# A two-layer graph network on one core: conv 1's weight product of the first graph in native float32, and another order of head and tail

## The chip, the cores and the metric

The kernel runs on one core of a Trainium2 chip. The metric is device time in microseconds (us) of one execution, here the median of three runs. The core has five engines that run side by side, each with its own instruction list, in order: TensorE (PE, matrix products into the PSUM banks; PEld is its loading of the stationary operand), VectorE (DVE), ScalarE (ACT), GpSimd (POOL) and SyncE (SP), which here only issues DMAs. They wait for one another by semaphores.

## The reference

There are 128 graphs of 128 nodes with 512 features (`x`), each with a 128x128 matrix `adj`. Two layers run one after the other.

```python
# layer 0
h = relu(layernorm(x))
x = x + (conv(layernorm(relu(conv(h, W1, b1))) * gamma + beta, W2, b2) + h)
# conv(h, W, b): H = (adj != 0); w = first row of adj
#   Dn = 1 / (H @ w);  Be = 1 / H.sum(axis=1)
#   Dn * (H @ (Be * (H.T @ (h @ W.T)))) + b
# layer 1
h = relu(layernorm(x))
x = x + relu(concat(h, (adj @ h) / rowsum(adj)) @ W.T)
```

W1 is 1024x512, W2 is 512x1024, W is 512x1024, all float32.

## The kernel before, in words

Each graph is one tile of 128 partitions, so the work is 128 graphs through a long pipeline of small steps. Each step is a Python function with the graph's number `g` (and sometimes a half), and issues one to some ten instructions. The order of the steps is written out by hand: `head()` lists the start, where graphs 0 to 4 enter and the weights are loaded and prepared; `step(s)`, for s from 3 to 124, is the steady loop, in which seven graphs stand at different points; `tail()` lists the end. The order of the list is the order in which each engine gets its instructions. An engine in front of an instruction that cannot start yet holds all that is behind it in its own list, and nothing else.

The steps that matter here, by graph:

- `load_x`, `load_adj`, `load_adjb`, `load_w1`, `load_w2`, `load_w3`, `load_bias` issue DMAs, all on SP except graph 0's `load_adjb`, which is on ACT. `load_adjb` loads adj in four pieces of rearranged 32x32 blocks. `load_affine` issues eight small DMAs on POOL.
- `incidence` (DVE: transpose, then not-equal), `incidence_count`, `incidence_weight`, `incidence_inverse`, `incidence_high` (ACT, then DVE, L419), `incidence_scale` (two parts), `node_matrix` (one matmul and ACT's copy) and `node_sum` (DVE) make the node operator S = H Be H^T of a graph, and its degrees. `node_floor`, `node_scale`, `node_up` make their inverse, in `dinv`.
- `x_sums`, `x_spread`, `scales`, `shifts`, `x_norm` are the layer norm of x, in `h0`; `residual` and `residual_bias` add to x on POOL.
- `conv1_nodes` multiplies S from the left, in native float32 (128 columns, eight instructions), into PSUM, `pz`.
- `conv1_high`, `conv1_low`, `conv1_rest` split `pz` into three parts `z`, and `conv1_weights(g, half)` multiplies by one half of W1. `conv1_main` (ACT) and `conv1_out` (DVE) take the two PSUM banks out into `r`, `conv1_bias` adds b1.
- `inner_sums`, `inner_spread`, `inner_norm` are the inner layer norm; `inner_out`, `inner_in`, `inner_turn` transpose `r` by way of DRAM (`n_scratch`, `nb`) and DVE; `inner_high`, `inner_low`, `inner_rest` split the result.
- `conv2_weights`, `conv2_main`, `conv2_weights_out`, `conv2_bias` (to `g`), `conv2_nodes` (to `py`), `conv2_out` finish layer 0. The `layer1_*`, `mean_*` and `aggregate` steps are layer 1, `finish` stores the graph.

Most products are split: a float32 value is written as a high and a low part in the format `fp32r`, and a third part `d` for the correction, so that one product takes three groups of matmuls (`product`, L521). Each half of a weight is a `Half`, 128 partitions x 4 x 512. `high(i)` (ACT, L179) and `low(i)` (DVE, L183) make the parts from the loaded values `raw`, two of the four blocks at a time, and `rest(i)` makes `d` from the two:

```python
            self.raw = const.tile([P, KD, 512], FP, tag=name + "d", name=name + "r")
...
                self.d = const.tile([P, KD, 512], FP, tag=self.name + "d", name=self.name + "d").bitcast(FR)
...
                eng.tensor_tensor(self.d[:, c], self.l[:, c], self.h[:, c], SUB)
```

So `d` takes the memory of `raw` (the same tag), and can be written only when `raw` has been read for the last time. On DVE `rest` is one instruction (L195), on POOL four, and without an engine it is a pair of matmuls with a unit matrix and a copy on ACT for each block (L199 to L201). The weights' names in the trace are `w10`, `w11`, `w20`, `w21`, `w30`, `w31`, with `r`, `h`, `l` or `d` behind them.

`beta_row(k)` (L262) is eight native float32 matmuls in all, of 512 columns, into one PSUM bank, which `beta_out` reads; `scale_w2(k)` then scales that block of W2 in place. `fill(768)` puts matmuls of 768 columns that nobody reads in front of the next use of a PSUM bank; in the head that is `conv1_nodes(0)`.

There are six PSUM banks for products, and two for `ps_s`, `pz` and `py`.

Of the kernel before, what the change touches and what calls it, by code (L numbers as in the profile page):

```python
# [7 lines left out]
FP = mybir.dt.float32  # L8
# [12 lines left out]
DOWN_12 = 2.0**-12  # L21
# [3 lines left out]
def gnn_kernel(  # L25
# [485 lines left out]

    @stage
    def conv1_low(g):
        PZ[g][0]()
# [430 lines left out]
    def head():  # L945
        load_w1(0, 0)
        load_adjb(0, nc.scalar)
        load_x(1)
        incidence(0)
        copy(eps_root, eps, AF.Sqrt)  # L950
        load_affine()
        load_x(0)
        incidence_weight(0, nc.gpsimd)
        incidence_count(0, nc.vector)
        load_w1(0, 1)
        incidence_inverse(0)
        x_sums(1, "A")
        x_sums(0)
        w1[0].high(0)
        w1[0].high(1)  # L960
        load_x(2)
        load_w1(1, 0)
        w1[0].low(0)
        incidence_high(0)
        x_spread(0)
        scales(0, 1)
        incidence_scale(0, 0, nc.gpsimd)
        incidence_scale(0, 1, nc.scalar)
        load_w1(1, 1)
        w1[0].low(1)  # L970
        w1[0].rest(1, nc.vector)
        load_adjb(1)
        shifts(0, 1, nc.gpsimd)
        x_norm(0)
        node_matrix(0)
        fill(768)
        w1[1].high(1)
        load_w2(0)
        node_sum(0)
        incidence(1)  # L980
        conv1_nodes(0)
        w1[1].high(0)
        residual(0)
        node_floor(0, nc.vector)
        incidence_count(1, nc.vector)
        load_adjb(2)
        w1[0].rest(0, nc.vector)
        x_spread(1)
        load_bias(b2_bc, b2)
        load_bias(b1_bc, b1)  # L990
        w1[1].low(1)
        incidence_inverse(1)
        conv1_high(0)
        conv1_low(0)
        conv1_rest(0)
        node_scale(0)
        incidence_weight(1, nc.gpsimd)
        conv1_weights(0, 0)
        incidence_high(1)
        w1[1].low(0)  # L1000
        incidence_scale(1, 0, nc.scalar)
        w1[1].rest(0, nc.vector)
        incidence_scale(1, 1, nc.scalar)
        load_adj(0)
        node_up(0, nc.scalar)
        conv1_main(0, 0)
        scales(1, 1)
        load_w2(1)
        node_matrix(1)
        shifts(1, 1, nc.gpsimd)  # L1010
        incidence(2)
        node_sum(1)
        incidence_count(2, nc.gpsimd)
        beta_row(0)
        conv1_out(0, 0)
        w1[1].rest(1, nc.vector)
        x_sums(2)
        beta_row(1)
        conv1_weights(0, 1)
        incidence_weight(2, nc.vector)  # L1020
        node_floor(1, nc.gpsimd)
        x_spread(2)
        scale_w2(0, nc.vector)
        scales(2, 1)
        x_norm(1)
        beta_row(2)
        load_x(3)
        shifts(2, 1, nc.gpsimd)
        incidence_inverse(2)
        conv1_bias(0, 0, nc.vector)  # L1030
        scale_w2(1, nc.scalar)
        w2[0].high(0)
        beta_row(3)
        incidence_high(2)
        conv1_nodes(1)
        load_adjb(3)
        scale_w2(2, nc.vector)
        conv1_main(0, 1)
        load_w3(1)
        mean_operator(0)  # L1040
        node_scale(1)
        scale_w2(3, nc.scalar)
        incidence_scale(2, 0, nc.vector)
        incidence_scale(2, 1, nc.scalar)
        w2[0].high(1)
        conv1_out(0, 1)
        residual_bias(0)
        conv1_high(1, True)
        node_matrix(2)
        conv1_bias(0, 1, nc.vector)  # L1050
        beta_row(4)
        beta_row(5)
        x_norm(2)
        node_sum(2)
        conv1_nodes(2)
        mean_degree(0, nc.vector)
        node_up(1, nc.gpsimd)
        node_floor(2, nc.vector)
        inner_sums(0)
        inner_spread(0)  # L1060
        residual(1)
        node_scale(2)
        residual(2)
        load_adjb(4)
        conv1_low(1)
        scale_w2(5, nc.vector)
        scale_w2(4, nc.vector)
        conv1_high(2)
        incidence(3)
        incidence_weight(3, nc.gpsimd)  # L1070
        conv1_rest(1)
        incidence_count(3, nc.gpsimd)
        scales(0, 2)
        incidence_inverse(3)
        conv1_low(2)
        beta_row(6)
        shifts(0, 2, nc.vector)
        beta_row(7)
        w2[1].high(0)
        conv1_rest(2)  # L1080
        incidence_high(3)
        w2[0].low(1)
        unit()
        scale_w2(6, nc.vector)
        inner_norm(0)
        x_sums(3)
        scale_w2(7, nc.scalar)
        w2[0].low(0)
        mean_inverse(0)
        w2[1].low(0)  # L1090
        node_up(2, nc.scalar)
        incidence_scale(3, 0, nc.vector)
        w2[1].high(1)
        conv1_weights(1, 0)
        conv1_weights(1, 1)
        incidence_scale(3, 1, nc.scalar)
        conv1_main(1, 0)
        conv1_main(1, 1)
        inner_out(0)
        w2[0].rest(0)  # L1100
        inner_in(0)
        conv1_out(1, 0)
        x_spread(3)
        w2[0].rest(1)
        conv1_out(1, 1)
        conv1_bias(1, 0, nc.vector)
        conv1_bias(1, 1, nc.vector)
        inner_sums(1)
        node_matrix(3)
        conv1_weights(2, 0)  # L1110
        scales(3, 1)
        incidence(4)
        w2[1].low(1)
        inner_spread(1)
        w2[1].rest(1, nc.gpsimd)
        incidence_weight(4, nc.vector)
        load_x(5)
        inner_turn(0)
        beta_out()
        scales(1, 2)  # L1120
        conv1_weights(2, 1)
        incidence_count(4, nc.gpsimd)
        inner_high(0)
        shifts(1, 2, nc.scalar)
        node_sum(3)
        inner_norm(1)
        w3[1].high(1)
        w3[1].high(0)
        load_x(4)
        shifts(3, 1, nc.gpsimd)  # L1130
        inner_low(0, nc.vector)
        load_w3(0)
        incidence_inverse(4)
        inner_rest(0)
        x_norm(3)
        w2[1].rest(0, nc.vector)
        incidence_high(4)
        conv2_weights(0)
        mean_scale(0, nc.scalar)
        conv1_nodes(3)  # L1140
        conv2_main(0)
        conv1_main(2, 0)
        conv1_main(2, 1)
        incidence_scale(4, 1, nc.scalar)
        inner_out(1)
        conv2_weights_out(0)
        conv1_high(3, True)
        inner_in(1)
        x_sums(4)
        residual_bias(1)  # L1150
        conv2_bias(0, nc.vector)
        conv1_out(2, 0)
        conv1_low(3)
        conv1_rest(3)
        incidence_scale(4, 0, nc.scalar)
        inner_turn(1)
        conv2_nodes(0)
        conv2_out(0)
        residual(3)
        w3[0].high(1)  # L1160
        load_adjb(5)
        residual_bias(3)
        x_spread(4)
        scales(4, 1)
        conv1_weights(3, 0)
        mean_out(0)
        inner_high(1)
        residual_bias(2)
        conv1_out(2, 1)
        layer1_sums(0)  # L1170
        conv1_bias(2, 0)
        conv1_bias(2, 1, nc.vector)
        layer1_spread(0)
        inner_low(1, nc.vector)
        scales(0, 3)
        shifts(0, 3, nc.vector)
        inner_sums(2)
        inner_rest(1)
        load_adj(1)
        w3[0].low(1)  # L1180
        shifts(4, 1, nc.gpsimd)
# [379 lines left out]
```

## Time and profile before

| | |
|---|---|
| median of 3 runs | 2447.64 us (2446.86 to 2447.76) |
| the profiled execution | 2447.67 us |
| its span, first to last instruction | 2445.9 us |
| busy: PE, PEld | 2422.7, 2009.6 us |
| busy: DVE, ACT, POOL | 2298.1, 2009.9, 1324.8 us |
| granted TensorE clock | 1.0 of full speed |
| first matmul | 11.40 us |
| first product of graph 0 | 16.88 us |
| first product of graph 1 | 31.94 us |
| first product of the steady loop | 70.94 us |
| one steady step | 18.75 us |
| last DMA issued | 2442.54 us |

In a row of the profile, `L530 PE MATMUL rm<-w10h,z` is a matmul of line 530, which writes `rm` and reads `w10h` and `z`; a number behind x counts instructions, and in an order of time the two first columns are start and length in us. Times of matmuls overlap, since they are pipelined: what counts is the distance from start to start. A wait is given as who waited, for whom, with the total, the count and the longest.

### The profile page before, as it was taken

The page shows a single profiled execution, that of the slowest core. Times are in us where ns is not written, and L with a number is a line of the kernel's source. Part 1 is how long each engine was busy: PE and PEld are TensorE (multiplying, and loading weights), DVE is VectorE, ACT ScalarE, POOL GpSimd, SP SyncE. Part 2 cuts the span into 40 slices and gives each one's busy share as a digit, 9 for nine tenths or more (in the row PEclk, how much of TensorE's full clock was granted, in tenths as well). Part 3 has the DMA queues.
Part 4 walks back from the last instruction along what each step waited for, and adds up shares of the span by engine and source line. Part 5 has one row for each costly group of instructions (what it writes and reads, how often), then busy time and mean ns, then how long its engine had stood idle before and what let it go on. Part 6 is the DMA issues. An engine that isn't in the chain of part 4 may idle for free.

```text
span 2445.9 us, 41647 instructions
## 1 busy us (share of the span) xinstructions
PE 2422.7 (99%) x11170; PEld 2009.6 (82%) x11170; DVE 2298.1 (94%) x5843; ACT 2009.9 (82%) x4512; POOL 1324.8 (54%) x1808
## 2 busy tenths in 40 slices
PE   7999999999999999999999999999999999999998
PEld 5788888888888888888888888888888888888886
DVE  8899999999999999999999999999999999999987
ACT  8888888888888888888888888888888888888785
POOL 5555555555555555555555555555555555555552
PEclk9999999999999999999999999999999999999999
DMA  6344433344434443444344443434343444344432
GB/s 186 114 129 125 130 124 129 124 130 128 129 119 130 132 126 123 129 129 127 124 128 128 126 129 123 132 123 130 122 133 121 130 127 131 119 131 131 127 124 92
DMA packets 408956, 311.39 MB, mean 127 GB/s; under 512 B 176656, under 2 KB 339984, under 8 KB 408720
## 3 DMA queue, kind: packets, MB, share of 16 engines
q1 hardware_dynamic: 407888, 308.66, 40.1%
q8 instruction: 88, 1.44, 0.2%
q14 instruction: 148, 1.21, 0.2%
q10 hardware_dynamic: 576, 0.07, 0.0%
q0 software_dynamic: 256, 0.01, 0.0%
HBM read 166.21 MB, written 142.34 MB: 126 GB/s over the span
## 4 chain that ended last, share of the span: by engine, by line
PE 95%; ACT 2%; DVE 1%; DMA 1%; issue 1%; SPq 0%; POOL 0%; POOLq 0%; DVEq 0%; ACTq 0%
PE gm L530 19%; PE rm L530 18%; PE am L530 9%; PE bm L530 9%; PE gd L535 9%; PE rd L535 9%; PE bd L535 5%; PE ad L535 5%; PE pz L488 4%; PE am L832 2%; PE ad L832 1%; PE ym L743 1%; PE yd L744 1%; PE ym L742 1%; PE ps_s L430 1%
## 5 line engine op out<-in xcount | busy, mean ns | idle before, releaser
L306 ACT ACTIVATE h<-x_t 128x512 f32<-128x512 f32 x255 | 159.1, 624 | 291.8 <-DVE x_t L754 283.8
L81 POOL TENSOR_TENSOR r<-r,b_bc 128x256 f32<-128x256 f32 x500 | 358.7, 739 | 70.1 <-DVE r L555 54.4
L300 POOL TENSOR_SCALAR st<-st 128x1 f32<-128x1 f32 x130 | 82.3, 633 | 569.9 <-DVE st L317 563.2
L81 POOL TENSOR_TENSOR hl<-ht,hh 128x256 fp32r<-128x256 f32 x250 | 235.4, 963 | 216.5 <-ACT hh L612 216.5
L81 POOL TENSOR_TENSOR x_t<-x_t,h 128x256 f32<-128x256 f32 x256 | 239.8, 959 | 1.3 <-ACT h L326 1.1
L81 POOL TENSOR_TENSOR g<-g,c 128x256 f32<-128x256 f32 x246 | 177.6, 743 | 72.4 <-DVE g L694 72.4
L326 ACT ACTIVATE h<-x_t,st 128x512 f32<-128x512 f32 x255 | 206.1, 808 | 2.0 <-POOL st L300 1.2
L555 DVE SCALAR_TENSOR_TENSOR r<-rd,dinv,r 128x512 f32<-128x512 f32 x256 | 190.8, 746 | 7.7 <-ACT r L550 6.3
L81 POOL TENSOR_TENSOR x_t<-x_t,b_bc 128x256 f32<-128x256 f32 x256 | 187.2, 752 | 0.0
L311 ACT ACTIVATE h<-x_t,st 128x512 f32<-128x512 f32 x255 | 182.9, 717 | 4.1
L550 ACT ACTIVATE r<-rm,dinv 128x512 f32<-128x512 f32 x256 | 174.7, 684 | 7.7 <-PE rm L530 4.4
L694 DVE SCALAR_TENSOR_TENSOR g<-gd,g 128x512 f32<-128x512 f32 x127 | 87.8, 691 | 79.5 <-issue 70.4
L621 DVE SCALAR_TENSOR_TENSOR nd<-nh,nl 128x1024 fp32r<-128x1024 f32 x127 | 155.5, 1225 | 4.2
L326 ACT ACTIVATE r<-r,st 128x1024 f32<-128x1024 f32 x128 | 157.8, 1233 | 0.1
L591 DVE STREAM_TRANSPOSE nt<-nb 128x1024 f32<-128x1024 f32 x127 | 156.9, 1235 | 0.4 <-DMA nb<-n_scratch 0.3
L81 DVE TENSOR_TENSOR nl<-nt,nh 128x1024 fp32r<-128x1024 f32 x127 | 153.5, 1208 | 1.9 <-ACT nh L612 1.7
L530 PE MATMUL am<-w31h,hh 128*128 128x512 f32 x504 | 146.8, 413 | 0.0
L311 ACT ACTIVATE junk<-r,st 128x1024 bf16<-128x1024 f32 x128 | 145.2, 1134 | 0.1
L488 PEld LDWEIGHTS pz<-s,h 128*128 128x128 f32 x1024 | 134.5, 192 | 11.1 <-ACT h L326 0.7
L530 PE MATMUL rm<-w11h,z 128*128 128x512 f32 x512 | 140.3, 396 | 0.0
L530 PE MATMUL rm<-w11l,z 128*128 128x512 f32 x512 | 139.3, 393 | 0.0
L530 PE MATMUL rm<-w10h,z 128*128 128x512 f32 x512 | 138.2, 392 | 0.9 <-ACT z L501 0.9
(244 smaller groups left out, 7594.1 us busy)
## 6 DMA issues: line engine op xcount, KB each, us to landing
n_scratch<-r SPq DMA_DIRECT2D x128, 512.0 KB, 2.6
nb<-n_scratch SPq DMA_DIRECT2D x508, 128.0 KB, 2.8
x_t<-in_x_dram SPq DMA_DIRECT2D x128, 256.0 KB, 2.7
h_scratch<-h SPq DMA_DIRECT2D x127, 256.0 KB, 2.3
hb<-h_scratch SPq DMA_DIRECT2D x508, 64.0 KB, 1.9
out_dram<-o SPq DMA_DIRECT2D x127, 256.0 KB, 2.0
adj_t<-in_adj_dram SPq DMA_DIRECT2D x128, 64.0 KB, 1.9
an_scratch<-adj_t SPq DMA_DIRECT2D x128, 64.0 KB, 1.6
```

What stands on the lines that cost most here:

```text
L81: eng.tensor_tensor(dst[:, s], a[:, s], b[:, s], op)
L306: copy(junk, src, func, accum_out=t[:, 0:1])
L311: copy(junk, src, AF.Square, bias=t[:, 1:2], accum_out=t[:, 2:3])
L326: copy(dst, src, func, bias=t[:, 5:6], scale=t[:, 4:5])
L488: nc.tensor.matmul(z[:, k * P : (k + 1) * P], H0[g][:, k * P : (k + 1) * P], S[g], start=True, stop=True)
L530: nc.tensor.matmul(pm, left[i](k), right(i, k), start=(i == 0 and k == 0), stop=(i == 1 and k == kk - 1))
L535: nc.tensor.matmul(pd, left[2](k), right(2, k), start=(k == 0), stop=(k == kk - 1), skip_group_check=True)
L550: copy(R[g][:, HALVES[half]], PY.pop((g, half)), AF.Copy, scale=DN[g][:, 1:2])
L555: nc.vector.scalar_tensor_tensor(r, PR.pop((g, half)), dn[:, 0:1], r, MUL, ADD)
L591: nc.vector.transpose(nt.rearrange("p k (i b) -> p k i b", b=B), t.rearrange("p i k a -> p k i a"))
L621: nc.vector.scalar_tensor_tensor(t, h, 2.0**-12, low, MUL, SUB)
L694: nc.vector.scalar_tensor_tensor(G[g], PG.pop(g), 4096.0, G[g], MUL, ADD)
```

## The change

Three functions are new. For graph 0 alone, `native_high` copies `pz` out once, as plain float32, scaled by 2^-12; `native_weights` multiplies it by a half of W1 as loaded (`raw`), four native float32 matmuls of 512 columns into one bank; `native_main` takes that bank out on ACT, with the row scale. They stand for `conv1_high`, `conv1_low`, `conv1_rest`, `conv1_weights`, `conv1_main` and `conv1_out` of graph 0. The four `rest` steps of W1 come behind the native product that reads their half. The parts of W1 are still made for all other graphs. `step(s)` is unchanged.

The order of the other steps in `head()` and `tail()` is new throughout, and some small steps sit on another engine. The diff, cut:

```diff
+    def native_high(g):
+        done.update((v.f, g) for v in (conv1_high, conv1_low, conv1_rest))
+        Z[g] = z = left.tile([P, KD, P], FP, tag="h1", name="z")
+        copy(z.rearrange("p k c -> p (k c)"), PZ.pop(g), AF.Copy, scale=DOWN_12)
+
+    def native_weights(g, half):
+        done.add((conv1_weights.f, g, half))
+        PR[g, half] = b = bank("rn")
+        for k in range(KD):
+            nc.tensor.matmul(b, Z[g][:, k], w1[half].raw[:, k], start=(k == 0), stop=(k == KD - 1))
+
+    def native_main(g, half):
+        done.update((v.f, g, half) for v in (conv1_main, conv1_out))
+        if half == 0:
+            R[g] = pool.tile([P, DH], FP, tag="r", name="r")
+        copy(R[g][:, HALVES[half]], PR.pop((g, half)), AF.Copy, scale=DN[g][:, 0:1])
```

The new head, from its start to the first product of graph 1, with the steps that the text speaks of:

```diff
     def head():
+        load_x(0)
         load_w1(0, 0)
         load_adjb(0, nc.scalar)
+        load_bias(b2_bc, b2)
+        incidence(0)
+        load_affine()
+        w1[0].high(0)
+        w1[0].low(0)
+        incidence_count(0, nc.vector)
+        x_sums(0)
         load_x(1)
...
+        load_w1(1, 0)
+        incidence_weight(0, nc.scalar)
+        scales(0, 1)
         load_w1(0, 1)
+        incidence_high(0)
+        shifts(0, 1, nc.vector)
+        incidence_scale(0, 0, nc.vector)
+        load_adjb(1)
+        incidence(1)
+        incidence_scale(0, 1, nc.scalar)
+        load_x(2)
+        w1[1].high(0)
+        load_w1(1, 1)
         w1[0].high(1)
+        node_matrix(0)
+        node_sum(0)
...
+        fill(768)
+        load_w2(0)
+        conv1_nodes(0)
+        native_high(0)
+        w1[1].high(1)
+        w1[0].low(1)
...
+        native_weights(0, 0)
+        w1[1].low(1)
+        w1[0].rest(0, nc.vector)
+        beta_row(0)
+        incidence_scale(1, 0, nc.scalar)
+        incidence(2)
...
+        beta_row(2)
+        native_weights(0, 1)
+        load_w2(1)
+        w1[0].rest(1, nc.vector)
+        beta_row(3)
+        load_adjb(3)
+        native_main(0, 0)
+        incidence_scale(2, 0, nc.scalar)
+        w2[0].low(0)
+        incidence_scale(2, 1, nc.vector)
+        native_main(0, 1)
+        scale_w2(2, nc.vector)
+        x_norm(2)
+        conv1_bias(0, 0, nc.vector)
+        shifts(1, 1, nc.gpsimd)
+        node_matrix(2)
+        node_sum(1)
+        x_norm(1)
+        conv1_bias(0, 1, nc.vector)
+        conv1_nodes(1)
+        inner_sums(0)
+        residual(2)
         w1[1].rest(0, nc.vector)
...
+        w1[1].rest(1, nc.gpsimd)
...
+        inner_norm(0)
+        unit()
+        inner_out(0)
...
+        beta_out()
         conv1_weights(1, 0)
         conv1_weights(1, 1)
```

Its end, and the places in the tail that the text speaks of:

```diff
+        conv2_weights(1)
...
+        w3[0].rest(1)
+        w3[0].rest(0, nc.gpsimd)
...
+        conv2_nodes(1)
...
+        inner_out(2)
+        inner_in(2)
         load_adjb(5)
         layer1_high(0)
         layer1_low(0, nc.vector)
+        load_adj(1)
+        w3[1].rest(1)
...
+        w3[1].rest(0)
...
     def tail():
...
-        layer1_low(c)
+        layer1_low(c, nc.vector)
...
-        layer1_trip_out(d)
-        mean_in(d)
...
-        layer1_trip_in(d)
+        layer1_trip_out(d)
...
+        layer1_trip_in(d)
...
+        mean_in(d)
...
-        mean_scale(e, nc.vector)
+        mean_scale(e, nc.gpsimd)
```

## The prediction

> **What bounds the kernel now.** I read the page's engine shares first, then the busy times in six stretches, then what TensorE waited for, and last the order of time in the head, the only place besides the tail that the change touches.
>
> The page:
>
> ```profile
> PE 2422.7 (99%) x11170; PEld 2009.6 (82%) x11170; DVE 2298.1 (94%) x5843; ACT 2009.9 (82%) x4512; POOL 1324.8 (54%) x1808
> PE 95%; ACT 2%; DVE 1%; DMA 1%; issue 1%; SPq 0%; POOL 0%; POOLq 0%; DVEq 0%; ACTq 0%
> ```
>
> TensorE is busy 99% and carries 95% of the chain. Time can only come from its 23.2 us without work, or go into more work for it. The stretches (columns: stretch, length, then busy time of PE, PEld, DVE, ACT, POOL, with instructions):
>
> ```profile
> 0.00:11.40 11.40, 0.00 (x0) 0.03 (x1) 2.64 (x10) 6.65 (x15) 6.36 (x15) 1.00 0.80 264
> 11.40:16.88 5.48, 4.54 (x14) 3.12 (x14) 5.32 (x10) 4.35 (x8) 3.51 (x4) 1.00 0.92 206
> 16.88:31.94 15.06, 14.72 (x57) 9.53 (x58) 14.15 (x38) 12.66 (x28) 6.74 (x12) 1.00 0.95 217
> 31.94:70.94 39.00, 36.79 (x156) 27.86 (x154) 35.34 (x62) 37.25 (x79) 19.27 (x28) 1.00 0.44 132
> 70.94:2395.15 2324.21, 2323.86 (x10768) 1936.94 (x10769) 2204.75 (x5661) 1922.87 (x4331) 1279.99 (x1739) 1.00 0.40 127
> 2395.15:2445.90 50.75, 42.80 (x178) 32.06 (x176) 35.86 (x66) 26.12 (x54) 8.88 (x13) 1.00 0.27 88
> ```
>
> 16.88 is the first product of graph 0, 31.94 the first of graph 1, 70.94 the first of the steady loop. From 70.94 to 2395.15 TensorE idles 0.35 us: nothing there can be won. The idle time lies in 0 to 16.88 (12.34), in the rest of the head (0.34 + 2.21) and after 2395 (7.95). In the head DVE (35.34 of 39.00) and ACT (37.25) are nearly as full as TensorE. Its waits, first in 0 to 120 us, then after 2250:
>
> ```profile
> PE ps_s L430 <- ACT sb L298: 11.4, 1, 11.4
> PE py L738 <- DVE g L81: 1.1, 1, 1.1
> PE rm L530 <- ACT z L501: 0.9, 1, 0.9
> ...
> PE py L738 <- POOL w11ds L81: 1.7, 1, 1.7
> PE py L738 <- DVE g L81: 1.0, 1, 1.0
> ```
>
> No product waited for a third part of W1. What the first product waits for is `z`, at the end of the chain adjacency, node matrix, x_norm, conv1_nodes. The durations that the sum uses:
>
> ```profile
> 2.69 1.28 ACT L950 ACT_TABLE_LOAD   x1 [2.69 <-issue]
> 9.52 1.23 DVE L183 SCALAR_TENSOR_TENSOR w10l<-w10h,w10r 128x1024 fp32r<-128x1024 f32 x1
> 11.75 2.76 PE L100 MATMUL pz<-eps 128*128 128x512 f32 x4
> 12.28 1.23 DVE L195 TENSOR_TENSOR w10d<-w10l,w10h 128x1024 fp32r<-128x1024 f32 x1
> 19.88 1.88 PE L262 MATMUL pc<-w20r,gb 128*128 128x512 f32 x4
> 22.53 1.08 PE L530 MATMUL rm<-w11l,z 128*128 128x512 f32 x4
> 23.45 1.09 PE L535 MATMUL rd<-w11d,z 128*128 128x512 f32 x4
> ```
>
> The x4 of L262 are two native matmuls of 512 columns, two instructions each; they start 0.43 apart. The x4 of L530 run from 22.53 to 23.45: 0.23 each.
>
> **The change part by part.**
>
> *The product.* Removed: 24 matmuls by 0.23 = 5.5 us. Added: 8 native ones, 16 instructions by 0.43 = 6.9. All of it is on TensorE's path: **+1.3** (1.1 to 1.6, by the last digits of the two spacings). TensorE's first 4 us run slower: the 512-column filler instructions start 0.85 apart, and conv1_nodes' spacing falls from 0.21 to 0.11 near 15.4. The new product starts after that, as the old one did. The Trainium skill (TensorE: Matmul & The Clock Gate, "What's actually happening") says that the array runs at half rate until a free-running window of about 3.4 us has been busy; by it another phase could leave part of the first native half at double spacing, up to 3.4 us more. This trace shows full speed 4.0 us after the first matmul, and the sum goes by that.
>
> *What goes with it.* DVE loses conv1_low and conv1_rest of graph 0 (0.67 each) and two conv1_out (0.74 each): 2.8 us. ACT's two copies out of PSUM stay (0.68 each). All other steps are the same, on other engines: w1[1].rest(1) (1.23 on DVE) goes to POOL and w2[1].rest(1) comes from POOL to DVE; two conv1_bias (0.67) leave DVE for POOL; small scalings move about. I count DVE 2.5 and ACT 2.0 less in the head, most of ACT's behind 32 us.
>
> *The start.* The x load, W1's quarter, b2 and the other x now stand ahead of the fourth piece of adjb. In the trace the pieces land in order of issue with the other loads (w10 1.5, x 0.65, b2 1.6 us of transfer), the last at 8.44. The new list ahead of it is 0.65 + 1.5 + 1.6 + 0.65 against 1.5 + 0.65 + 0.65 + 1.6: equal, so incidence(0) starts near 8.5 again. Behind it DVE now does w1[0].low(0) (1.2) before the count and the inverse, where before it stood behind them, ahead of L419; and scale(0,0) is a DVE 0.28 instead of a POOL 1.24. Together node_matrix(0) comes at 11.3 (11.40 before). ACT then does two W1 high parts (0.95 each, start to start) ahead of the node matrix's copy and x_norm(0), which ends at 13.8 (before 13.25); the filler ends at 14.2 anyway, so that costs nothing while the filler covers it; without it, 0.5. conv1_nodes 1.5 and z's copy 0.6 put the product at 16.5: **-0.4** (-0.8 if adjb lands earlier; +1.0 if ACT's table is loaded twice, once for the copies now in front of the square root: row 1.28, of which some 0.3 is slack). The Trainium skill (ScalarE: Activation LUTs, "What ACT_TABLE_LOAD costs") prices a switch of table set at about 2.7 us, of which 1.28 is the load. By it the start would be 2.0 later. The trace has one load only, and the page also lists copy among the functions of every set.
>
> *From the product to graph 1's (15.06 before).* A new wait: w1[0].rest(0) writes over the raw half, so it waits for native_weights(0, 0), which ends at 16.5 + 3.4 = 19.9, while DVE is through with w1[1].low(1) near 18. Queued behind it are incidence(2), mean_operator(0), incidence_inverse(2), scales(2, 1); node_matrix(2) and x_norm(2) wait for those. The 1.8 us of idle DVE is covered by the 2.8 that it lost. Then TensorE: beta_row 0.86, node_matrix(1), two beta_rows, the second half 3.4, a beta_row: 26.9. ACT, replayed by these rows, comes to x_norm(1) only at 28.2, behind two sums, two spreads, scale_w2, w2[0].high(0) and the two native copies, so conv1_nodes(1) waits 1.3, where before 0.7 was lost on node_matrix(2): **+0.6**, between -0.7 (no loss) and +2.0. Two conv1_nodes and four beta_rows later graph 1's product starts at 33.4 (31.94 before).
>
> *From there to the loop (39.00 before).* 2.21 us of idle and some slow starts were lost to DVE and ACT: 1.1 before conv2_nodes(0), the rest on banks before and between the W2 and W3 third parts. With ACT 2.0 shorter, beta_out ahead of graph 1's products (its bank free by 33, at 44.4 before) and the W3 parts split around conv2_nodes(1), I take back **-1.4**: about two thirds of the idle, the row that all of it comes from. Ends: -2.2 and +1.5. The upper one holds the late loads: load_adjb(5) and load_adj(1) now stand behind inner_in(2) on SP (issued 69.85 to 71.6 before), would land near 75.3, and incidence(5) stood at 75.17; inner_low(2), behind it on DVE, had 0.7 of slack.
>
> *The tail.* TensorE's order is nearly the same. layer1_low(c) goes from POOL (1.45) to DVE (0.69), and TensorE stood for its output: -0.5. trip_in(d) no longer stands behind mean_in(d), whose four issues took 2.9 on SP: -0.4. The 1.7 for conv2_bias(e) on POOL stays. **-0.9**; ends -2.0 (the 7.95 less the last 5.5, in which only the final chain runs) and +1.5 (mean_scale(e) goes to POOL, and mean_transpose(e) had some 1.5 us to spare).
>
> **Sum.** +1.3 - 0.4 + 0.6 - 1.4 - 0.9 = -0.8, taken as -1.0 with the late digits. The profiled execution took 2447.67 (span 2445.9), which is the median 2447.64 within 0.03; so 2446.7. Changes under 0.2% (4.9 us) are not told from none here.
>
> **The rivals.** *Graph 0 comes late* (slower). The vectors of graph 0 share one chain: native copy, bias, sums, spread, inner_norm(0), trip through DRAM, conv2_weights(0). Before, inner_norm(0) ended at 35.1 and conv2_weights(0) began with 0.1 us of wait. ACT's list between z's copy and inner_norm(0) is 16.1 us of work; from 16.5 with the waits above I get 34.7. Past 36.5 (35.1 plus graph 1's later start) every us goes on TensorE. If the waits for native products cost ACT 8 us instead of 2, it ends near 41: +4.5 - 0.8 + 2, so 2453.4. For it: ACT's queue is strict and x_norm(2), x_norm(1) now stand ahead of inner_sums(0). Against: no wait of 2 us in ACT's list before.
>
> *All gains come in* (faster): -0.8 + 1.1 - 0.7 - 2.2 - 2.0 = -4.6, so 2443.0. For it: each of these is idle time that the stretches show. Against: DVE and ACT are 90% and 96% full in the head, and gaps seldom all close.
>
> *The table is loaded twice or the first transfers come late*: the start at +1.0 instead of -0.4: 2448.1. Against: the first 5 us of ACT are empty.
>
> *The change is no change for TensorE*: were a native product as short as the split one, 1.3 less: 2445.4; L262 speaks against it.
>
> **How the numbers follow.** Forecast 0.62, graph 0 late 0.18, all gains 0.10, start late 0.08, no added work 0.02. Faster takes four fifths of all gains: 0.08. Slower takes four fifths of graph 0 late and a little of the forecast's upper ends: 0.16. Same 0.76. Range: 2443.2 leaves out about 0.08, 2451.5 about 0.12.
>
> **What would show it.** Right: 16 native instructions 0.43 apart for graph 0; first product near 16.5; graph 1's near 33.4; the loop's first layer1_mean near 70.8; the 18.75 us step unchanged; TensorE idle after the loop under 7.5. Wrong: a second ACT_TABLE_LOAD, DVE idle over 2 us in front of w10d, inner_norm(0) ending after 36.5, or a wait of TensorE inside the loop.

## The result, and the profile after

The changed kernel takes 2453.85 us (median of 10 runs, 2452.07 to 2456.06), before beside it 2447.71 (10 runs, 2446.27 to 2450.16). The ratio is 1.0024 with a 95% interval of 1.0016 to 1.0032, so the change costs 3.9 to 7.8 us. The forecast was 2446.7, a little faster than before, with a range of 2443.2 to 2451.5. The profiled execution of the changed kernel took 2453.32 us (span 2451.5), 5.65 more than the profiled execution of before.

Lines after `L515` have moved by 17: `L530` of before is `L547`, `L535` is `L552`, `L550` is `L567`, `L738` is `L755`. First the page of the changed kernel, engine shares and chain:

```profile
PE 2426.5 (99%) x11162; PEld 2007.7 (82%) x11162; DVE 2300.3 (94%) x5854; ACT 2009.2 (82%) x4508; POOL 1318.2 (54%) x1797
PE 94%; ACT 2%; DVE 2%; DMA 1%; issue 0%; SPq 0%; POOL 0%; DVEq 0%; ACTq 0%
```

Then the six stretches between the same events as before (start, node matrix of graph 0, first product of graph 0, first product of graph 1, loop, end; columns as before):

```profile
0.00:11.66 11.66, 0.00 (x0) 0.00 (x0) 2.67 (x11) 7.21 (x17) 4.73 (x12) 1.00 0.70 214
11.66:17.09 5.43, 4.74 (x13) 3.17 (x13) 3.62 (x9) 3.45 (x7) 2.85 (x4) 1.00 0.96 265
17.09:34.34 17.25, 15.88 (x51) 7.96 (x51) 14.14 (x36) 14.78 (x35) 11.71 (x13) 1.00 0.93 205
34.34:74.88 40.54, 37.60 (x157) 27.47 (x155) 37.62 (x69) 36.00 (x72) 21.84 (x31) 1.00 0.43 126
74.88:2400.79 2325.91, 2325.38 (x10768) 1936.91 (x10769) 2205.27 (x5664) 1921.65 (x4328) 1267.78 (x1728) 1.00 0.40 127
2400.79:2451.51 50.72, 42.89 (x178) 32.14 (x176) 36.96 (x68) 26.13 (x55) 9.27 (x12) 0.98 0.28 88
```

Read the second column against that of before: 11.66 for 11.40, 5.43 for 5.48, 17.25 for 15.06, 40.54 for 39.00, 2325.91 for 2324.21, 50.72 for 50.75. So the head costs 3.9 us, the loop 1.7 in these two executions, the tail nothing. TensorE's idle time between graph 1's product and the loop has grown from 2.21 to 2.94. DVE and ACT, which were expected to have less work in the head, are busy 37.62 and 36.00 us there, for 35.34 and 37.25. TensorE's waits in 0 to 120 us (who, for whom, total, count, longest):

```profile
PE ps_s L430 <- ACT sb L298: 11.7, 1, 11.7
PE py L755 <- DVE g L81: 1.7, 2, 1.1
PE pz L488 <- ACT h L326: 1.4, 1, 1.4
PE rn L521 <- ACT z L515: 0.7, 1, 0.7
PE gm L547 <- DVE nl L81: 0.3, 1, 0.3
```

The order of time shows the native product and, behind it, the 1.37 us that conv1_nodes(1) waited for x_norm(1). Of the next stretch it shows ScalarE's 2.14 us without work in front of conv1_main(1, 0):

```profile
17.09 3.70 PE L521 MATMUL rn<-w10r,z 128*128 128x512 f32 x8 [0.69 <-ACT z L515]
23.47 3.60 PE L521 MATMUL rn<-w11r,z 128*128 128x512 f32 x8
29.41 0.82 PE L488 MATMUL pz<-s,h 128*128 128x128 f32 x5 [1.37 <-ACT h L326]
40.67 1.27 ACT L567 ACTIVATE r<-rm,dinv 128x512 f32<-128x512 f32 x2 [2.14 <-PE wd L199]
```

That last row is the lead. conv1_main(1, 0) writes over `r`, which inner_out(0) reads. The bracket names a matmul that had long been done; the other thing it waits for is the DMA of inner_out(0), issued at 35.57 and landed at 40.59. In before the same trip was issued at 35.16 and landed at 37.75.

### The profile page after: what moved, and what is told of

It is laid out like the page before. It is cut to its first block, busy times and chain, and to the rows that moved or that the text cites. A ratio compares the mean times of both kernels' runs of the same rounds, so it can differ in the third digit from the quotient of the medians.

```text
span 2451.5 us, 41621 instructions
## 1 busy us (share of the span) xinstructions
PE 2426.5 (99%) x11162; PEld 2007.7 (82%) x11162; DVE 2300.3 (94%) x5854; ACT 2009.2 (82%) x4508; POOL 1318.2 (54%) x1797
## 4 chain that ended last, share of the span: by engine, by line
PE 94%; ACT 2%; DVE 2%; DMA 1%; issue 0%; SPq 0%; POOL 0%; DVEq 0%; ACTq 0%
PE gm L547 18%; PE rm L547 18%; PE am L547 9%; PE bm L547 9%; PE gd L552 9%; PE rd L552 9%; PE bd L552 5%; PE ad L552 5%; PE pz L488 4%; PE am L849 2%; PE ad L849 1%; PE ym L760 1%; PE ym L759 1%; PE yd L761 1%; PE ps_s L430 1%
## 5 line engine op out<-in xcount | busy, mean ns | idle before, releaser
L567 ACT ACTIVATE r<-rm,dinv 128x512 f32<-128x512 f32 x254 | 173.2, 683 | 13.7 <-DMA n_scratch<-r 5.2
L547 PE MATMUL am<-w31h,hh 128*128 128x512 f32 x504 | 146.6, 413 | 0.0
L547 PE MATMUL rm<-w11h,z 128*128 128x512 f32 x508 | 139.6, 396 | 0.0
L547 PE MATMUL rm<-w11l,z 128*128 128x512 f32 x508 | 138.1, 393 | 0.0
L488 PE MATMUL pz<-s,h 128*128 128x128 f32 x1024 | 135.5, 276 | 1.4 <-ACT h L326 1.4
```

Of the source, the lines that this page charges most:

```text
L488: nc.tensor.matmul(z[:, k * P : (k + 1) * P], H0[g][:, k * P : (k + 1) * P], S[g], start=True, stop=True)
L547: nc.tensor.matmul(pm, left[i](k), right(i, k), start=(i == 0 and k == 0), stop=(i == 1 and k == kk - 1))
L567: copy(R[g][:, HALVES[half]], PY.pop((g, half)), AF.Copy, scale=DN[g][:, 1:2])
```

## The experiments

The kernels were timed in five rounds, in four groups, each beside before on the same chip (before: 2449.6, 2449.4, 2449.1 and 2448.8 us). An interval is about 2 us to either side, so the small terms are read from the profiled executions. The start, up to graph 0's first product, differs by up to 1.6 between them (16.26 to 17.88 us). "Head" is therefore counted from graph 0's first product to the loop: 54.07 us in before and 54.02 in a second execution, 57.79 and 57.86 in the changed kernel.

(In the stretches above, graph 1's product is put 0.03 earlier than its first matmul in before, 31.97, so 15.06 and 39.00 there are 15.09 and 38.98 here.)

**Which part of the change.** Four kernels took the change apart. First, the native product alone, in the order of before:

```diff
-        conv1_high(0)
-        conv1_low(0)
-        conv1_rest(0)
...
+        native_high(0)
...
-        conv1_weights(0, 0)
+        native_weights(0, 0)
```

with native_main for conv1_main, no conv1_out of graph 0, and W1's third parts behind the product.

> Head and tail in the order of before, only graph 0's product native, and W1's third parts behind it. Theory A (the new order of the head costs the time; the product only its 1.3 us on TensorE, with 2.8 us of DVE work gone): 2448.2 to 2449.8 against 2447.7, first product of graph 0 within 0.3 of 16.88, first product of the loop at 71.0 to 73.0. Rival B (the native product, or the third parts waiting behind it, costs the time): 2452 or more, first product of the loop at 74 or later.

Measured: 2453.12 us, ratio 1.0016 (1.0007 to 1.0025), so about +3.5, between the two theories. Its head takes 56.39, 2.32 more than before, and all of that lies between graph 0's product and graph 1's (17.47 instead of 15.09); from there to the loop it is as before (38.92). TensorE's product is 1.4 longer. The rest goes with a wait of 1.6 in front of graph 2's node matrix, for ScalarE's copy of graph 1's `z`; in before the wait at this place was 0.3. (A second wait for a copy of `z`, 1.5 where before had 0.9, lies ahead of graph 0's product and outside this count.)

The new head with the tail of before:

> The changed head with the tail of before. Theory A (all of it in the head, the tail is worth nothing): 2453 to 2454.5, first product of the loop at 74.5 to 75.3. Rival C (the new tail loses what its listing should win): 2451.5 or less, with the same head. If the new tail wins the 0.9 us that were forecast: 2454.5 to 2455.

2454.77 us, 1.0018 (1.0009 to 1.0027), about +5.2, where theory A begins at +5.3: the cost is there without the new tail. The loop starts at 73.46, a us earlier than theory A had it, and the head takes 56.66; the table further down shows a shorter trip in this execution.

The head of before with the new tail:

> The head of before with the changed tail. Theory A: 2447.3 to 2448.2, the loop as before (step 18.75 us, first product of the loop at 70.95). Rival C: 2449.5 or more. If the new tail wins the forecast 0.9 us: 2446.8.

2449.58 us, 1.0000 (0.9991 to 1.0009): no effect of the tail shows, to about 2 us. From graph 118's layer1_mean to the end this kernel's profiled execution takes 161.5 us, before 160.9 and, in its second one, 161.6.

The changed kernel has a second table load in ScalarE's list, which before has not:

```profile
7.27 1.28 ACT L974 ACT_TABLE_LOAD   x1
```

The fourth kernel takes it away, by the square root in front of the first copy:

```diff
         load_affine()
+        copy(eps_root, eps, AF.Sqrt)
         w1[0].high(0)
...
-        copy(eps_root, eps, AF.Sqrt)
```

> The changed kernel with the square root of eps as ACT's first activation, so that one table load is left. If the second load of 1.28 us sits on the path of the start: first matmul at 10.9 to 11.2 instead of 11.66, first product 0.6 to 1.0 earlier than 17.09, time 2452.9 to 2453.3. If the adjacency's last piece (8.34) and DVE's low part set the start anyway: first matmul 0.1 to 0.3 earlier, first product 16.8 to 17.0, time 2453.6 to 2453.9.

2455.01 us, 1.0023 (1.0014 to 1.0032). The second load is gone, but the node matrix comes at 12.19, not earlier. In this execution the last piece of adjacency came late: DVE's transposition behind it starts at 9.16, in the changed kernel at 8.47. Counted from there the node matrix comes 3.03 us later, and so it does (3.02 or 3.03) in six executions of the new head that have the second load. The 1.28 us are off the path.

So the cost is in the head, part of it with the product, part with the new order.

**The price of TensorE's time.** Before, with 1.28 us of filler work inside the head:

```diff
+        fill(384)
         conv1_weights(0, 0)
...
+        fill(384)
         conv1_weights(0, 1)
```

> The kernel before, with 1.28 us of filler work for TensorE inside its head (384 columns of native float32 ahead of each half of graph 0's weight product) and nothing else. It prices the first term of the sum by itself. Theory A (extra work of TensorE costs what it lasts): +1.3 us, ratio 1.0005, and the loop's first layer1_mean 1.3 later, 72.2 instead of 70.95. Theory B (in a head where VectorE and ScalarE are nearly full, late work of TensorE is passed on and grows): +3 us or more, as the product alone did (+3.5). Theory C (the head has slack in which it vanishes): 0 to +0.5.

2449.27 us, 1.0000 (0.9991 to 1.0009); the head takes 54.66, 0.59 more. The first filler runs from 15.59 to 16.48, in the time in which TensorE would have waited for `z`, and vanishes (theory C). The second, 0.64 us of work with no such wait beside it, comes out as 0.59 (theory A). Nothing grew (theory B). So e1's 2.32 cannot be put down to the 1.4 of longer work alone; that its waits make up the rest is read from its trace, and no run took them away.

**The two waits in the changed kernel.** First graph 0's rows in a buffer of their own:

```diff
-            R[g] = pool.tile([P, DH], FP, tag="r", name="r")
+            R[g] = left.tile([P, DH], FP, tag="t3", name="r2")
```

in native_main alone.

> The changed kernel, with graph 0's rows r in a buffer of their own, so that ScalarE's conv1_main(1, 0) need not wait until inner_out(0) has landed. Theory A (that wait, 2.1 us of idle ScalarE after a trip of 5.0 us, is where the term of -1.4 turned into +1.5): conv1_main(1, 0) starts near 38.5 instead of 40.67, the loop starts 1.0 to 2.0 earlier (73 to 74 instead of 74.88), and the time falls by as much, ratio to the kernel before 1.0016 or less. Theory B (the stretch is set by VectorE, or by the trip itself through inner_in(0) and conv2_weights(0)): ScalarE starts earlier, but the loop starts within 0.4 of 74.88.

2454.52 us, 1.0017 (1.0008 to 1.0026). conv1_main(1, 0) starts at 38.98 instead of behind the landing (40.98), as wanted, but the loop starts at 74.82 and the head takes 57.41: theory B. ScalarE's idle time was a symptom. What is left of theory B's two candidates, the vector engines or the trip, is settled further down.

Then x_norm(1) in front of the native copy, and what it needs ahead of it:

```diff
         scales(1, 1)
+        shifts(1, 1, nc.vector)
...
+        node_sum(1)
+        x_norm(1)
         native_main(0, 1)
         scale_w2(2, nc.vector)
         x_norm(2)
         conv1_bias(0, 0, nc.vector)
-        shifts(1, 1, nc.gpsimd)
         node_matrix(2)
-        node_sum(1)
-        x_norm(1)
```

> The changed kernel, with x_norm(1) ahead of native_main(0, 1) and x_norm(2), shifts(1, 1) on VectorE directly behind scales(1, 1), and node_sum(1) ahead of them. It takes away the 1.37 us that conv1_nodes(1) waited. Theory A (each of TensorE's waits in the head is on the path that sets the end): conv1_nodes(1) near 28.0 instead of 29.41, graph 1's product near 33.0 instead of 34.34, the loop 1.0 to 1.4 earlier. Theory B (from graph 1's product to the loop the trip of graph 0 and the two vector engines set the end): graph 1's product comes earlier, the loop starts within 0.4 of 74.88.

2452.98 us, 1.0014 (1.0005 to 1.0022). Four rows of its order of time:

```profile
20.72 1.09 PE L262 MATMUL pc<-w20r,gb 128*128 128x512 f32 x2 [0.76 <-DMA w20r<-in_w2t_dram]
23.48 3.60 PE L521 MATMUL rn<-w11r,z 128*128 128x512 f32 x8
27.90 1.06 PE L488 MATMUL pz<-s,h 128*128 128x128 f32 x8
33.22 1.48 PE L547 MATMUL rm<-w10h,z 128*128 128x512 f32 x4
```

The second half of graph 0's product starts where it did (23.48, changed 23.47), and graph 1's product comes 1.12 earlier (33.22 for 34.34): theory A, for 1.1 of the 1.37. The loop starts at 72.48, 2.40 earlier. The other 1.28 lie behind graph 1's product, where the trip of inner_out(0) also got shorter (3.25 us instead of 5.01), which this edit does not touch. The head takes 56.22, only 1.57 less, because graph 0's product had come 0.8 early in this execution (16.26). That gained nothing: beta_row(0) behind it waited until 20.72 for the first half of W2.

**What makes the trip long.** TensorE's instructions come as 16 KB packets of their own queue, one about every 27 us in the loop. In the changed kernel one starts 1.0 us behind the issue of the trip. The DMA view from 35 to 41.5 us (40 slices of 0.16 us), then the queue of that packet, then the trip:

```profile
DMA  2000000049999997936789750000000000000000
GB/s 42 0 6 0 0 0 0 0 176 479 378 403 403 403 378 176 277 63 114 189 340 416 303 189 0 25 25 25 25 25 25 25 25 25 25 0 0 0 0 0
q8 instruction: 1, 0.02, 1.8%
n_scratch<-r SPq DMA_DIRECT2D x1, 512.0 KB, 5.0
```

From 39.1 to 40.7 us the transfers run at 25 GB/s, a sixteenth of the 403 before, which reads as one of the 16 DMA engines still moving its share of the trip when the others are done. The code load took 1.90 us, on one engine. The same view of before has no such end (its own code load begins at 38.31, after the landing):

```profile
DMA  0000008999999800000030002799863113587885
GB/s 0 0 0 0 0 0 353 429 403 403 429 429 454 328 0 0 0 0 0 0 101 0 6 13 69 246 334 303 252 214 114 25 57 76 176 265 227 284 258 202
n_scratch<-r SPq DMA_DIRECT2D x1, 512.0 KB, 2.6
```

The kernel f4 lengthened TensorE's stream by 16 instructions, to that of before, and h4 is the same again:

```diff
     def head():
+        FILL.extend([1] * 4)
         load_x(0)
```

> The changed kernel, with four native matmuls of one column each ahead of the first node matrix, while TensorE has nothing to do. TensorE's stream of instructions gets as long as in the kernel before (the native product takes 16 instructions fewer, weight loads included), so its 16 KB code loads fall on the same instructions of the loop again; nothing else changes. Theory A (the 1.5 us that the changed kernel loses in the loop come from code loads that meet a trip through DRAM, and where they meet is set by the lengths of the engines' streams): the loop from graph 1 to graph 118 loses about 2.0 us over its usual step again, instead of 3.5, and the time falls by 1 to 1.5 us; the code load that lay in inner_out(0) at 36.6 moves about 1.7 earlier, still into the trip. Theory B (something else, or chance from run to run): the loss stays at 3 to 4.5 us.

> The kernel of f4_pe_code_phase again: the changed kernel with TensorE's stream as long as in before. Theory A: 2.0 to 2.6 us lost in the loop again. Theory B: anything from 2 to 5. From the first product to the loop 57.6 to 57.9 in either.

2453.65 us, 1.0019 (1.0010 to 1.0028), and 2454.33, 1.0023 (1.0014 to 1.0032). In the head the code load still falls 1.0 and 1.1 us behind the issue, and the trips take 4.94 and 4.80. Twelve such matmuls move it away:

```diff
+        FILL.extend([1] * 12)
```

> The changed kernel with twelve native matmuls of one column each at TensorE's idle start (48 instructions with their weight loads, where f4 had 16). The code load that begins 1.0 us behind the issue of inner_out(0) should come at an earlier instruction, 3 us or more before the trip. Theory A (the code load makes the trip long, the trip sets conv2_weights(0) and the loop): the trip of inner_out(0) takes 2.6 to 3.3 us instead of 5.0, conv1_main(1, 0) starts within 0.2 of the landing, and the loop's first layer1_mean comes 0.9 to 1.4 earlier counted from graph 0's first product (56.4 to 56.9 instead of 57.8). Theory B (the trip is long for another reason, load_x(4) behind it on its queue for one): it stays at 4.4 or more, the loop at 57.4 to 57.9. Loop: another phase of TensorE's code loads; the steps that are long move to other numbers.

2451.58 us, 1.0013 (1.0004 to 1.0021). The code load is at 31.66, before the trip. The same DMA view, from 35 to 41.5 us; no q8 is in it:

```profile
DMA  3100000009999999979759962001349668989879
GB/s 62 15 4 6 0 0 0 0 0 378 429 429 429 403 403 378 202 176 114 164 202 403 391 265 76 0 0 32 69 158 227 233 189 258 347 296 309 290 252 284
q1 hardware_dynamic: 932, 1.28, 61.2%
n_scratch<-r SPq DMA_DIRECT2D x1, 512.0 KB, 2.9
```

The slow end is gone, the trip takes 2.89 us and the head 56.12: 1.67 less, with nothing changed but twelve matmuls of one column. Theory A holds. The other way round was tried on before, with five such matmuls:

> The kernel before with five such matmuls at TensorE's idle start (20 instructions): the code load at 38.3, 3.1 behind the issue of inner_out(0), should come some 10 matmuls earlier, into the trip. Theory A: if it begins less than 1.5 us behind the issue, the trip takes 3.5 to 5 us instead of 2.6 and conv2_weights(0) and the loop come up to 1.4 later (counted from the first product 54.5 to 55.5 instead of 54.07); if it does not come to lie there, the trip stays at 2.6 and the loop at 54.0 to 54.2. Theory B: a code load that lies in the trip leaves it at 2.6. The loop has another phase of code loads: its long steps move to other numbers.

2450.09 us, 1.0004 (0.9995 to 1.0013). The code load moved to 31.71, ahead of the trip; the trip takes 2.65, the head 54.07. So a code load inside this trip was never seen with the order of before, and the reverse of h1 is not shown. All 18 profiled executions together:

| executions | code load behind the issue of inner_out(0) | it took | trip |
|---|---|---|---|
| before, h3, e3, e1 | 3.1 to 3.6 us, after the landing | | 2.59 to 2.60 |
| f1, g3, h2 (order of before) | none in the trip | | 2.59 to 2.65 |
| h1, g2 (new head) | none in the trip | | 2.89, 2.87 |
| f3, e2, g1 | 0.25, 0.61, 0.44 | 0.93, 1.09, 1.43 | 3.25, 3.63, 3.94 |
| e4, h4, f2 | 1.26, 1.14, 0.94 | 1.01, 1.55, 1.86 | 4.39, 4.80, 4.87 |
| f4, changed, g4 | 1.00, 1.00, 1.11 | 1.84, 1.90, 1.84 | 4.94, 5.01, 5.06 |

The length of the code load alone does not order the trips (e4's is shorter than e2's). Its end does: in all nine executions with one, the trip lands 1.9 to 2.1 us after the code load has ended. load_x(4), the other cause that theory B of h1 names, is issued 0.39 behind the trip in every execution of the new head, so by itself it can stand for no more than the 0.2 to 0.3 by which h1 and g2 lie above f1, g3 and h2. e2 has the changed kernel's head to the letter; with a trip 1.4 shorter, its head is 1.1 shorter.

**W3's third parts.** On the base of f3, they stand as in before:

```diff
-        w3[0].rest(1)
+        w3[1].rest(1)
+        w3[1].rest(0)
...
         load_adj(1)
-        w3[1].rest(1)
+        w3[0].rest(1)
...
-        w3[1].rest(0)
```

> The kernel of f3_x_norm1_first, with W3's third parts in the order of before around conv2_nodes(1): both quarters of half 1 ahead of it and the quarter w3[0].rest(1) behind it, where the changed kernel has one quarter ahead and two behind. From conv2_weights(0) to the loop f3 took 25.96 us (before 24.90, changed 26.15). Theory A (the split of W3's third parts is what costs the last microsecond of that stretch: TensorE lost 2.6 to 2.7 us there between the copies of ScalarE and conv2_nodes(1), before 1.8): 24.9 to 25.2, the loop's first layer1_mean 0.8 to 1.0 earlier than f3 counted from graph 0's first product (55.3 instead of 56.2). Theory B (that microsecond is the late trip or the vector engines, wherever the third parts stand): 25.7 or more.

2452.33 us, 1.0011 (1.0002 to 1.0020). From conv2_weights(0) to the loop 25.24 instead of 25.96; the head 55.68, though its trip was 0.7 longer than that of f3. Theory A. A second pair, both without a code load in the trip, agrees: 25.47 in h1 with the changed order, 24.68 in g2 with that of before. First three rows of the changed kernel's order of time, then two of g1's, then three of before:

```profile
70.19 0.40 PE L200 MATMUL wd<-w30h,unit 128*128 128x512 f32 x1
71.22 1.10 PE L755 MATMUL py<-g,s 128*128 128x512 f32 x2 [0.64 <-DVE g L81]
73.46 0.49 PE L199 MATMUL wd<-w31l,unit 128*128 128x512 f32 x1 [0.22 <-ACT w31d L201]
```

```profile
70.42 0.39 PE L200 MATMUL wd<-w31h,unit 128*128 128x512 f32 x1
70.65 1.02 PE L755 MATMUL py<-g,s 128*128 128x512 f32 x2
```

```profile
68.21 0.50 PE L199 MATMUL wd<-w31l,unit 128*128 128x512 f32 x1 [0.22 <-ACT w31d L201]
68.55 0.39 PE L200 MATMUL wd<-w31h,unit 128*128 128x512 f32 x1
68.78 1.02 PE L738 MATMUL py<-g,s 128*128 128x512 f32 x2
```

With only one quarter ahead of it, conv2_nodes(1) came too early and stood 1.03 us behind its neighbour (1.04 in f3, 1.03 in h1); in before, g1 and g2 it is 0.23. The wait of 0.22 for a copy of ScalarE between two quarters is there in before too.

**An early filler.** TensorE is slow at its start in every execution. Nine matmuls of filler in its idle first 11 us, on g1 and on before:

```diff
     def head():
+        FILL.extend([512] * 9)
```

> g1 with nine more filler matmuls of 512 columns native ahead of the first node matrix, where TensorE has nothing to do (from about 0.9 us to about 10.5). Theory A (TensorE's slow first 3 to 4.4 us of work after its start, in the records of all runs, are a matter of how long it has been working): conv1_nodes(0) runs at 0.11 us spacing from its first matmul, the filler of 768 columns behind the node matrix takes 1.3 instead of 2.5, so conv1_nodes(0) starts when x_norm(0) is done and the first product starts 0.5 to 1.4 earlier for the same node matrix (4.0 to 4.3 behind it, where before had 5.5, changed 5.4 and f3 4.7); the rest as g1. Theory B (the slow start belongs to the first use after the transfers, not to idle time): the spacings stay, the start stays.

> The kernel before with the same nine filler matmuls at its start and nothing else: what the early filler is worth without the native product. Theory A: the first product 4.0 to 4.3 behind the node matrix instead of 5.5, and the time 0.5 to 1.2 us lower, as far as VectorE has the third parts of W1 ready (conv1_rest(0) and w1[0].rest(0) end near 18.2 in before, the product's third part is read from 18.7). Theory B: no change. If the changed kernel's product needs less of VectorE at that point, g2 gains more of the early start than g3.

g2: 2452.39 us, 1.0013 (1.0005 to 1.0022); the first product comes 4.60 behind the node matrix, not quite the 4.0 to 4.3, since x_norm(0) is later than the filler. What the early product gains is lost right behind it: beta_row(0) waits 1.13 for the first half of W2, as in f3. The trip is free of a code load (2.87) and the head takes 55.32. g3: 2449.58 us, 1.0001 (0.9993 to 1.0010), a miss: the product starts 5.48 behind the node matrix as before, because z's copy has to wait for its turn on ScalarE. Its head takes 55.40, 1.3 more than before's, since the product then ran slowly at first (last section). No version of these beats before.

**The loop.** The changed kernel and before, unaltered, a second time:

> The changed kernel itself, unaltered, next to the others. Theory A (the 1.5 us lost inside the loop belong to the kernel): the loop from graph 1 to graph 118 loses 3 to 4.5 us over its usual step again. Theory B (they differ from one execution to the next, as the times of one kernel do by some 5 us): it may lose anything from 2 to 5, and the sum of head and loop moves with the time of the execution. The ratio to the kernel before stays near 1.0024 either way; the start may move by 0.5 to 0.8 with the place at which TensorE's records turn from slow to fast.

> The kernel before, unaltered, for a second profiled execution. Theory A (the loss inside the loop belongs to the kernel's phase of code loads): 2.0 to 2.5 us over the usual step from graph 1 to 118 again (changed kernel 3.5 and 5.6), with long steps at graphs 5, 11, 21, 37, 53, 69, 85, 117. Theory B (chance of the execution): anything from 2 to 5, in line with its time.

2453.98 us, 1.0019 (1.0009 to 1.0028), and 2448.84, 0.9998 (0.9989 to 1.0007). Loss is what graph 1 to graph 118 take over 117 steps of 18.7465:

| kernel | time of this execution | head | loss in the loop |
|---|---|---|---|
| before | 2447.67 | 54.07 | 2.03 |
| before again (h3) | 2451.24 | 54.02 | 4.65 |
| changed | 2453.32 | 57.79 | 3.51 |
| changed again (g4) | 2456.43 | 57.86 | 5.64 |
| code load phase of before (f4) | 2452.63 | 57.72 | 2.20 |
| the same again (h4) | 2454.74 | 59.20 | 2.77 |
| third phase (h1) | 2449.84 | 56.12 | 1.40 |

The loss does not repeat: before alone gives 2.03 and 4.65. So the 1.5 to 1.7 us between the two first profiles can't be put down to the change (theory B). Some of the long steps do belong to the kernel: they lie at graphs 5, 11, 21, 53 and 117 in both executions of before, at 8, 14, 24, 37, 79, 88, 94 and 105 in both of the changed kernel. So do TensorE's code loads: in before one comes 9.5 to 9.6 us into graphs 5 and 21, in the changed kernel 9.7 into 8 and 24, and in f4 and h4, with the stream as long as in before, at graphs 5 and 21 again. But the code load alone does not make the step long: step 5 takes 18.75 us, the usual time, in both f4 and h4. Whether their phase also sets a mean loss is open: the three low values above are few, and two other kernels with a lengthened stream lost 5.23 (g2) and 5.45 (h2).

## Why the prediction was wrong, by its steps

*The product, +1.3*: right. 16 instructions 0.43 apart, 8 times 0.43 = 3.43 us for each half, 6.9 for 5.5.

*The start, -0.4*: it came out at +0.2 (17.09 for 16.88), and at +0.7 in the second executions (17.88 in g4 for 17.18 in h3). The second table load, which the rival *The table is loaded twice* named, was there, but e4 shows that it cost nothing; ScalarE's next instruction starts at 8.57, right behind the 1.28 us of the load, so of the 2.7 that the prediction gives for a switch of table set no more is to be seen. The node matrix stands between 10.97 and 11.83 in the seven executions with the order of before, between 11.49 and 12.39 in the eleven with the new head, so the new head is later at this point by some 0.4. About half of it lies behind DVE's transposition of graph 0's adjacency: from there the node matrix comes 2.83 later in four of the seven and 3.02 or 3.03 in seven of the eleven. What sets either half was not tried. A product at 16.5 would have gained little in any case: in f3 and g2 beta_row(0) behind it waited for the first half of W2 until 20.72 and 21.41, and in the changed kernel it started at 20.63.

*From the product to graph 1's, +0.6 beside the 1.3*: nearly right. conv1_nodes(1) waited 1.37 where 1.3 was forecast, on the same ScalarE list, and the stretch is 17.25 long where 16.9 was forecast. f3 confirms that this wait was on the path, for 1.1 of the 1.37.

*From there to the loop, -1.4*: **this is the step that failed**, by 2.9 us: it was +1.5. I took the idle time of before as something to be won back and priced neither of two things that put it back. First, the trip of inner_out(0) was taken as 2.6 us because the trace of before shows 2.6; but there the code load lay half a us behind its landing, and the new head moved trip and code load against each other. With the load taken out, graph 1's product to the loop is 38.88 (h1) and 38.98 in before: 1.66 of the 2.9. Second, the split of W3's parts around conv2_nodes(1), which I counted among the gains, cost 0.7 (g1 against f3) or 0.8 (h1 against g2). With both out, in g2, the stretch takes 38.00, 1.0 less than in before, so most of the 1.4 was there; g2 has x_norm(1) first and the early filler as well. The half us that is left of the 2.9 was not traced. The room on the vector engines that I had counted with was not there either: up to the loop, by the first four stretches, the changed kernel has DVE busy 58.05 us for 57.45 and ACT 61.44 for 60.91 (1.28 of it the second table load), where I had 2.5 and 2.0 less. The wait of conv2_nodes(0), 1.1 in before, was still 1.1.

*The tail, -0.9*: nothing came (50.72 for 50.75). TensorE's order there is nearly the same and so are its waits after 2250 us, 1.7 for POOL and 1.0 for DVE:

```profile
PE py L755 <- POOL w11ds L81: 1.7, 1, 1.7
PE py L755 <- DVE g L81: 1.0, 1, 1.0
PE bm L547 <- DVE hl L81: 0.2, 1, 0.2
```

I credited layer1_low and trip_in with what they gained by themselves. The view of before shows no wait of TensorE for the output of either; the 0.2 for `hl`, which layer1_low writes, is new.

*The loop, 0*: right as far as the runs can tell. One execution of each kernel differs from another by more than the 1.5 to 1.7 at issue. But the 0.35 us of idle time, from which I took that nothing could be won in the loop, does not show what the long steps lose, 2.03 us in the same execution.

The rival *Graph 0 comes late* gave 2453.4, almost what was measured, but not by its mechanism. inner_norm(0) ended at 35.55, before its limit of 36.5, and ScalarE's list was not late. Graph 0 became late one step further on, in its trip: that the number fits is luck. Of the signs of being wrong that the prediction names, only the second table load stood out, and it was harmless; DVE stood 1.17 us in front of w10d, under the 2 us. None of them looked at the trip.

The head is 3.7 us longer, from graph 0's product on. With x_norm(1) first, W3's parts as before and no code load in the trip, all in g2, 1.25 of it is left. That is close to the product's own work, but it is made of other pieces: 2.23 more up to graph 1's product, with the wait of 1.13 for W2 in it, and the 1.0 less behind. The interval of 3.9 to 7.8 (2.2 to 6.9 in g4's group) holds the 3.9 to 4.5 by which the loop starts later (74.88 for 70.95, and 75.74 in g4 for 71.20 in h3); whether another us or two belongs to the change in the mean is not settled.

## What to carry to other kernels

A trip through DRAM whose landing sets the next stage must be priced with a margin for what else lands on the DMA engines, TensorE's own code among it: in this kernel twelve matmuls of one column moved it, and took 1.7 us off the head. Idle time in a trace is no stock of gain: name for each us the wait that ends it, and what ends next. Before a loss in a loop is given to a change, profile the same kernel twice.

## What the runs showed of the hardware

Code loads share the DMA engines with data: one 16 KB packet of 0.9 to 1.9 us, on one engine of 16, stretched a 512 KB trip from 2.6 (2.9 in the new head) to as much as 5.06 us. The trip landed 1.9 to 2.1 us after the packet had ended, so both when the packet began and how long it took count.

TensorE's slow phase depends on the execution, and can come back. In h4 it was slow from the node matrix at 11.49 through conv1_nodes, then stood 0.7, and ran the first four instructions of the native product 0.85 apart instead of 0.43. That made h4's head 1.5 longer than that of f4, the same kernel:

```profile
17.03 5.47 PE L521 MATMUL rn<-w10r,z 128*128 128x512 f32 x8 [0.69 <-ACT z L515]
```

5.47 us stand here for the 3.70 of the changed kernel. In g3 TensorE had run at full spacing (eight matmuls of conv1_nodes in 1.16), stood 1.92 for ScalarE, and then started the product at 0.43 for 0.23:

```profile
14.22 1.16 PE L488 MATMUL pz<-s,h 128*128 128x128 f32 x8 [0.75 <-DVE s L438]
17.30 2.07 PE L530 MATMUL rm<-w10h,z 128*128 128x512 f32 x4 [1.92 <-ACT z L501]
```

The Trainium skill (TensorE: Matmul & The Clock Gate, "What's actually happening") puts the turn at a free-running window of about 3.4 us, so that it differs from run to run. The rows agree that it differs, by more than the half us to either side that the section names: 4.0 us behind the node matrix in before, 9.1 in h4. The page speaks of one idle window of that length before the slow rate returns; in g3 some 2 us without a matmul were followed by it. The prediction's doubt on this point, that part of the first native half could run at double spacing, came true in h4 alone.
